# Folding attention vectors on TensorE, with ScalarE and TensorE in a written order, in a four-layer graph-attention kernel

## The chip, the cores and the metric

The kernel runs on one core of one Trainium2 chip. The metric is the device time of one execution in microseconds (us). A core has TensorE (PE: matrix products into PSUM), VectorE (DVE: elementwise work and reductions), ScalarE (ACT: functions of one operand, with a scale and a bias), GpSimd (POOL: elementwise work, and the issue of indirect DMAs, "gathers") and SyncE (SP: here only issues DMAs). Each engine runs its own list of instructions in order and waits on semaphores for the others. 16 DMA engines move data between HBM and SBUF.

## What is computed

There are 3327 nodes with 512 features and a sparse symmetric adjacency matrix with some 17 neighbours to a row. Four layers follow one another, each a layer norm with a ReLU, and a graph attention whose output is added to x. The first one, cut to what matters:

```python
h = jnp.maximum(_layernorm(x, axis=-1), 0.0)
h = (h @ W.T).reshape(n, 8, 64)                    # 8 heads of 64
e_src = jnp.einsum('nhd,hd->nh', h, a_src)
e_dst = jnp.einsum('nhd,hd->nh', h, a_dst)
e = leaky_relu(e_src[:, None, :] + e_dst[None, :, :], 0.2)
alpha = softmax(where(mask[:, :, None], e, -inf), axis=1)
x = x + jnp.einsum('ijh,jhd->ihd', alpha, h).reshape(n, 512)
```

The other layers differ in heads (4, 1, 8), in an elu, and in whether a node always attends to itself. The scores e_src and e_dst are linear in the normalised input, so the kernel "folds" the attention vectors into the weights: column j of W times a_src, summed over a head, is one more column of the weight matrix. A projection of 512 + 16 columns then gives features and scores at once.

## The kernel before, in words

Rows are padded to 3328 and cut into 26 tiles of 128 (`NT`).

**The list stage** (`tile_gat_stack`, lines 526 to 791) turns the dense adjacency matrix into neighbour lists, and projects all tiles for layer 0. For each tile t:

- SP loads the adjacency tile `a` (128x3328 int32, 1664 KB; three buffers; L697). GpSimd multiplies it by descending column numbers into `key` (L698; three buffers).
- VectorE adds a bonus to the diagonal (L702) and takes the 8 largest of each of 16 segments (L707). Between these it works off `pieces` of the tile before: the 40 largest overall (L662, L664), the count held (L635, `counted`), its one-hot row (L640, `sorted_in`), and later the place within it (L654, `placed`).
- ScalarE sums the adjacency tile (L704), copies the list out (L632, L633), and centres the row tile x of 128x512 with its variance (`centred_by_scalar`, L488 to L495). The row tile `vx` (five buffers) is loaded from ScalarE's own DMA queue (L726).
- TensorE turns the centred tile (`turned`, L454), ScalarE cuts it (`cut`, L461), TensorE projects it into `pv` (`projected`, L472; one PSUM buffer), GpSimd takes the root of the variance (`rooted`, L434), ScalarE scales `pv` by it into `vx` (L683, L685), and SP stores that row tile (528 KB) in the table `tabx` (L687). In `features` all of it is called for tile t-1 at the end of step t.
- TensorE also sums the one-hot rows into running counts (L642 to L646), which ScalarE copies to `sofar` (L649) for the next tile.

In step 1 the weights of layer 0 are loaded (`Weights`, L382 ff.), and all eight folds follow at once on VectorE: a product `prod` of 128x512 (L408) and a reduction of it (L410) each. The folds read the attention vectors broadcast over 128 partitions (`av`, L395).

```python
with tc.manual_schedule(engines={Pool, DVE}):
    for t in range(NT):
        ...
        if t == 1:
            while W.left:
                W.fold()
```

What sets the order: inside `manual_schedule` the engines named keep the order of the program text. The others (here ScalarE, TensorE and SP) are ordered by the compiler's own scheduler. After the last tile, VectorE ranks the rows by their counts (L738 to L750), and TensorE builds lists of gather indices (L789) with `low` and `spare` as scratch; `low` lives from the stage's start and is not used until then.

**The layers** (`tile_gat_lists`) go over tiles in steps of up to four neighbours (`GROUP`). In layer 0, each step's neighbours are gathered from `tabx` by GpSimd (L838), five steps ahead (`LOOK`, buffers `g`). `scored` makes the attention weights (L892 to L908), `group` multiplies features by them on VectorE (L931) and sums on TensorE (L936). A finished tile is normed, turned and projected by the weights of the next layer (L472). The next layer's weights `W` are folded on VectorE in steps 0, 1 and 2 of layer 0, three at a time (L1436 to L1438), and those of the layer after are loaded at step 16 of a layer.

Of the kernel before, what the change touches and what calls it, by code (L numbers as in the profile page):

```python
# [10 lines left out]
F32 = mybir.dt.float32  # L11
U8 = mybir.dt.uint8
BF16 = mybir.dt.bfloat16
I32 = mybir.dt.int32
AF = mybir.ActivationFunctionType
# [3 lines left out]
P = 128  # L19
# [361 lines left out]
class Weights:  # L381

    def __init__(self, nc, pool, work, l, ws, avs):
        F = ws[l].shape[0]
        HF, KC = F // 2, F // P
        self.l, self.H, self.D = l, HEADS[l], F // HEADS[l]
        self.nc, self.work, self.HF = nc, work, HF
        self.w = pool.tile([P, KC, 2, HF + 8], F32, name="w")  # L390
        self.av = pool.tile([P, 2, F], F32, name="av", bufs=1)
        for s in range(2):
            nc.sync.dma_start(self.w[:, :, s, :HF],
                              ws[l][:, s * HF:(s + 1) * HF].rearrange("(k p) n -> p k n", p=P))
            nc.sync.dma_start(self.av[:, s, :], bass.AP(tensor=avs[l].tensor, offset=avs[l].offset + s * F,  # L395
                                                        ap=[[0, P], [1, F]]))
        if self.H < 8:
            nc.vector.memset(self.w[:, :, :, HF + self.H:], 0.0)
        self.left = [(s, k) for s in range(2) for k in range(KC)]

    def fold(self):

# [46 lines left out]
def turned(nc, xn, ident, ps_t):  # L449

    KC = xn.shape[1] // P
    pt = ps_t.tile([P, KC, P], F32, name="pt")
    for k in range(KC):
        nc.tensor.transpose(pt[:, k, :], xn[:, k * P:(k + 1) * P], ident)  # L454
    return pt


def cut(nc, pt, work):

    hT = work.tile(list(pt.shape), F32, name="hT")  # L460
    nc.scalar.activation(hT, pt, AF.Relu)  # L461
    return hT


def projected(nc, W, hT, ps_v):

    KC = hT.shape[1]
    HF = KC * P // 2
    pv = ps_v.tile([P, 2, BANK], F32, name="pv")
    for s in range(2):  # L470
        for k in range(KC):
            nc.tensor.matmul(pv[:, s, :HF + 8], hT[:, k, :], W.w[:, k, s, :],  # L472
                             start=(k == 0), stop=(k == KC - 1))
    return pv
# [50 lines left out]


@with_exitstack
def tile_gat_stack(ctx: ExitStack, tc: tile.TileContext, x, adj, adjT, ws, avs, out):

# [32 lines left out]
    with ExitStack() as c1:  # L564
# [16 lines left out]

        fixed = ps_k.tile([P, BANK], F32, name="fixed")
        ahead, boost, bins, one = fixed[:, :P], fixed[:, P:2 * P], fixed[:, 2 * P:2 * P + BINS], fixed[:, 298:299]
        nc.scalar.activation(boost, ident, AF.Copy, scale=BOOST)
        ones = once.tile([P, P], F32, name="ones")
        upper = once.tile([P, P], F32, name="upper")
        limit = once.tile([P, BINS], F32, name="limit")
# [50 lines left out]
        def sorted_in(t):  # L638
            nonlocal sofar, count
            nc.vector.tensor_scalar(o[:, t, :], bins, held[:, t:t + 1], None, OP.is_equal)  # L640
            pn = ps_n.tile([P, BANK], F32, name="pn", bufs=1)
            nc.tensor.matmul(pn[:, :BINS], upper, o[:, t, :], start=True, stop=False)  # L642
            nc.tensor.matmul(pn[:, :BINS], ident, sofar, start=False, stop=True)
            count = ps_n.tile([P, BANK], F32, name="count", bufs=1)[:, :BINS]
            nc.tensor.matmul(count, ones, o[:, t, :], start=True, stop=False)
            nc.tensor.matmul(count, ident, sofar, start=False, stop=True)  # L646
            if t < NT - 1:
                sofar = once.tile([P, BINS], F32, name="sofar", bufs=2)
                nc.scalar.activation(sofar, count, AF.Copy)  # L649
            return pn  # L650

        def placed(t, pn):
# [24 lines left out]
            nc.vector.tensor_tensor(m1, own, L[:, :, 0], OP.not_equal)  # L677
            nc.vector.tensor_reduce(wrong[:, 1:2], m1, AX.X, OP.add)

        def features(t, vx, xn, ve):  # L680
            pv = projected(nc, W, cut(nc, turned(nc, xn, ident, ps_t), work), ps_v)
            rstd = rooted(nc, ve, small, half)
            nc.scalar.activation(vx[:, :ROW].rearrange("p (s n) -> p s n", s=2), pv[:, :, :ROW // 2], AF.Copy,  # L683
                                 scale=rstd)
            nc.scalar.activation(vx[:, ROW + F:].rearrange("p (s n) -> p s n", s=2), pv[:, :, ROW // 2 - 8:ROW // 2],  # L685
                                 AF.Copy, scale=rstd)
            nc.sync.dma_start(tabx[t * P:(t + 1) * P, :], vx)  # L687

        rows = [once.tile([P, 2 * ROW], F32, name=f"vx{i}") for i in range(5)]
        count, pieces, last, normed = None, [], None, None  # L690
        with tc.manual_schedule(engines={mybir.EngineType.Pool, mybir.EngineType.DVE}):
            for t in range(NT):
                a = apool.tile([P, NP], I32, name="a")
                key = kpool.tile([P, NP], I32, name="key")
                quarter = NP // 4 if t == 0 else NP
                for c in range(0, NP, quarter):
                    nc.sync.dma_start(a[:, c:c + quarter], adj[t * P:(t + 1) * P, c:c + quarter])  # L697
                    nc.gpsimd.tensor_tensor(key[:, c:c + quarter], a[:, c:c + quarter], keys[:, c:c + quarter], OP.mult)  # L698
                if t == 1:
                    W = Weights(nc, wpool, work, 0, ws, avs)  # L700
                dg = key[:, t * P:(t + 1) * P]
                nc.vector.tensor_add(dg, dg, boost)  # L702
                waste = once.tile([P, NP], mybir.dt.bfloat16, name="waste")
                nc.scalar.activation(waste, a, AF.Relu, accum_out=total[:, t:t + 1])  # L704
                cand = small.tile([P, SEGS * 8], F32, name="cand")
                for g in range(SEGS):
                    nc.vector.max(cand[:, g * 8:(g + 1) * 8], key[:, g * SEG:(g + 1) * SEG])  # L707
                    if g == SEGS // 2 and last is not None:
                        last()
                        last = None  # L710
                    elif g > 0 and pieces:
                        pieces.pop(0)()
                if t == 0:
                    constants()
                if t == 1:
                    while W.left:
                        W.fold()
                if t == 2:
                    own = late_constants()
                if t > 0:  # L720
                    last = then
                pieces, then = rest(t, cand)

                vx = rows[t % 5]
                xt = vx[:, ROW:ROW + F]
                nc.scalar.dma_start(xt, x[t * P:(t + 1) * P, :])  # L726
                if normed is not None:
                    features(*normed)
                normed = (t, vx, *centred_by_scalar(nc, xt, small, work))
            features(*normed)  # L730
            pieces[4:4] = [last]
            for piece in [*pieces, check, then]:
                piece()

        with tc.manual_schedule(engines={mybir.EngineType.Pool, mybir.EngineType.PE,
                                         mybir.EngineType.DVE, mybir.EngineType.Activation}):
# [63 lines left out]
def tile_gat_lists(ctx: ExitStack, tc: tile.TileContext, x, adj, ws, avs, out, ident, half, slots, L, low, spare, tabx, tabs):  # L800
# [48 lines left out]
    class Tile:  # L849


        def __init__(self, l, t, W):
            self.l, self.t, self.W = l, t, W

            first = GROUP - 1 if l == 0 else GROUP
            self.k0 = [0] + list(range(first, CAPS[t], GROUP))
            self.own = first - 1 if l == 0 else 0
            self.groups = []
# [138 lines left out]
        def cut(self):  # L997
            if self.W is not None:
                self.hT = cut(nc, self.pt, work)
# [365 lines left out]
    for l in range(NL):  # L1365
# [3 lines left out]
        with ExitStack() as c2:  # L1369
# [47 lines left out]
            for s in range(-1, at_end):  # L1417
                def do(place):
                    for piece in at.pop((s, place), []):
                        piece()  # L1420
                while fetched < min(len(steps), s + LOOK):
                    steps[fetched][0].fetch()
                    fetched += 1
                do("first")
                if s + 1 < len(steps):
                    steps[s + 1][0].scored(steps[s + 1][1])
                do("scored")
                if 0 <= s < len(steps):
                    tl, i = steps[s]
                    tl.group(i)  # L1430
                    if i == len(tl.k0) - 1:
                        tl.finish(s)
                do("last")
                if s == 16 and l + 2 < NL:
                    following = Weights(nc, wpool, work, l + 2, ws, avs)
                if l == 0 and s in (0, 1, 2):  # L1436
                    for _ in range(3):
                        W.fold()  # L1438
                if s >= 24 and s % 4 == 0 and following is not None:
                    following.fold()  # L1440
            scatter()
# [43 lines left out]
```

## Time and profile before

| what | us |
|---|---|
| median of 3 runs (lowest, highest) | 2424.75 (2415.73, 2427.66) |
| profiled execution: its own time | 2419.54 |
| its span, first to last instruction | 2417.8 |
| list stage: last key product ends | 241.1 |
| list stage: DMA of the ranks issued | 256.7 |
| first gather of layer 0 | 271.2 |

| engine | busy us | share |
|---|---|---|
| PE (products) | 2068.3 | 86% |
| DVE | 1885.1 | 78% |
| POOL | 1739.5 | 72% |
| ACT | 936.3 | 39% |

How to read what follows: a line of the timeline has start, duration, engine, line of the kernel, operation, output and input with shapes, and in brackets how long the engine sat idle ahead of it and what ended that. A line of waits has engine and line that waited, what it waited for, the sum in us, how often, and the longest. A line of the windows has busy us of PE, PE's weight loads, DVE, ACT and POOL in a stretch, the granted TensorE clock, the share of time that the DMA engines were busy, and GB/s. "SPq" and "ACTq" are DMA issues. The granted TensorE clock was 0.953 over the span.

### The profile page before, as it was taken

What the parts mean: (1) busy time and instruction counts of PE and PEld (TensorE: products, weight loads), DVE (VectorE), ACT (ScalarE), POOL (GpSimd) and SP (SyncE); (2) the same over time, 40 slices, a digit from 0 to 9 for tenths busy, and PEclk for the clock granted to TensorE, in tenths of its full rate; (3) what the DMA queues carried; (4) which work ended last, traced back from release to release, by engine and by line L of the source; (5) the groups of instructions that cost most, each with busy time, mean ns of one, the idle gap of its engine ahead of it and who ended that gap; (6) DMA issues with size and microseconds to landing.
All of it is one profiled execution on the core that took longest, in us unless ns stands there. A gap on an engine that the chain in (4) does not pass through costs nothing.

```text
span 2417.8 us, 27489 instructions
## 1 busy us (share of the span) xinstructions
PE 2068.3 (86%) x7298; PEld 1197.0 (50%) x7298; DVE 1885.1 (78%) x4857; ACT 936.3 (39%) x2528; POOL 1739.5 (72%) x1717
## 2 busy tenths in 40 slices
PE   2778779888988885898999987899898699999997
PEld 1656334444444432454455544456565465556653
DVE  7988788877777763888888884888878578888886
ACT  5777113434331111433333332544443444344430
POOL 7899267777777776766677772778778467777775
PEclk9988899999999997999999998999999899999999
DMA  5887569999998788887888884889887578888885
GB/s 227 316 299 248 153 192 299 276 299 282 286 283 237 234 231 241 242 245 235 234 261 255 256 237 141 270 262 283 268 248 240 161 226 256 250 243 246 252 241 176
DMA packets 260732, 594.23 MB, mean 246 GB/s; under 512 B 103699, under 2 KB 121107, under 8 KB 256214
## 3 DMA queue, kind: packets, MB, share of 16 engines
q0 software_dynamic: 124368, 432.13, 59.5%
q1 hardware_dynamic: 132454, 153.45, 19.6%
q10 hardware_dynamic: 3744, 6.82, 0.8%
q8 instruction: 59, 0.97, 0.2%
q14 instruction: 107, 0.88, 0.1%
HBM read 542.60 MB, written 49.65 MB: 245 GB/s over the span
## 4 chain that ended last, share of the span: by engine, by line
DVE 31%; DMA 17%; PE 16%; issue 13%; POOL 12%; ACT 9%; DVEq 0%; SPq 0%; ACTq 0%; POOLq 0%
DVE m L931 13%; POOL g L838 8%; DMA g<-tab,idxb 6%; PE bank L936 5%; DMA g<-tabx,twiceb 4%; PE pv L472 4%; PE whole L1173 3%; POOL key L698 3%; DVE bank L924 3%; ACT r L1280 2%; DMA g<-tab,idxa 2%; DVE room L1296 2%; DVE z L902 2%; ACT pw L903 2%; DVE z L900 1%
## 5 line engine op out<-in xcount | busy, mean ns | idle before, releaser
L936 PE MATMUL bank<-m,ident 128*128 128x512 f32 x2414 | 1128.0, 613 | 144.8 <-DVE m L931 144.3
L838 POOL DMA_INDIRECT g<-tab,idxb x712 | 683.1, 959 | 236.0 <-issue 162.0
L931 DVE TENSOR_TENSOR m<-g,pw 128x512 f32<-128x512 f32 x1207 | 752.2, 682 | 100.2 <-ACT pw L903 99.6
L936 PEld LDWEIGHTS bank<-m,ident 128*128 128x128 f32 x2414 | 448.7, 194 | 689.2 <-issue 314.6
L472 PE MATMUL pv<-w,hT 128*128 128x264 f32 x1664 | 431.5, 413 | 67.8 <-ACT hT L461 44.5
L903 ACT ACTIVATE pw<-z 128x32 f32<-128x32 f32 (+4 forms) x356 | 68.2, 191 | 988.9 <-DVE z L902 988.9
L472 PEld LDWEIGHTS pv<-w,hT 128*128 128x128 f32 x1664 | 331.7, 203 | 166.8 <-ACT hT L461 50.8
L838 POOL DMA_INDIRECT g<-tab,idxa x297 | 286.3, 964 | 165.0 <-issue 110.6
L838 POOL DMA_INDIRECT g<-tabx,twiceb x342 | 324.0, 947 | 106.0 <-issue 79.5
L1173 PE MATMUL whole<-ve,em 128*128 128x512 f32 x468 | 217.8, 612 | 16.3 <-DVE em L1152 11.2
L698 POOL TENSOR_TENSOR key<-a,keys 128x3328 int32<-128x3328 int32 (+1 forms) x29 | 189.3, 6530 | 16.3 <-DVE cand L707 11.8
L924 DVE SCALAR_TENSOR_TENSOR bank<-g,L,bank 128x512 f32<-128x512 f32 x243 | 183.3, 754 | 6.8
L900 DVE TENSOR_TENSOR z<-g,pw 128x32 f32<-128x32 f32 (+4 forms) x356 | 62.6, 176 | 152.1 <-DMA g<-tabx,twiceb 64.7
L1314 PEld LDWEIGHTS whole<-L,room 128*128 128x128 f32 x1248 | 147.5, 190 | 24.9 <-issue 19.1
L838 POOL DMA_INDIRECT g<-tabx,twicea x99 | 94.9, 959 | 78.5 <-issue 38.1
L1314 PE MATMUL whole<-L,room 128*128 128x130 f32 x1248 | 147.8, 274 | 0.0
L707 DVE MAX8 cand<-key 128x8 f32<-128x208 int32 x416 | 144.0, 364 | 0.1
L1173 PEld LDWEIGHTS whole<-ve,em 128*128 128x128 f32 x468 | 88.1, 196 | 109.2 <-issue 87.2
L1280 ACT ACTIVATE r<-low,L 128x384 f32<-128x384 f32 x208 | 121.2, 583 | 5.1
L454 PE MATMUL pt<-ident,xn 128*128 128x128 f32 x416 | 65.4, 281 | 35.4 <-ACT hT L461 13.6
L454 PEld LDWEIGHTS pt<-ident,xn 128*128 128x128 f32 x416 | 52.5, 145 | 68.6 <-issue 28.3
L931 DVE TENSOR_TENSOR bank<-g,pw 128x512 f32<-128x512 f32 x74 | 51.5, 696 | 37.4 <-ACT pw L903 36.6
(180 smaller groups left out, 2192.6 us busy)
## 6 DMA issues: line engine op xcount, KB each, us to landing
a<-in_adj SPq DMA_DIRECT2D x25, 1664.0 KB
tab<-v SPq DMA_DIRECT2D x78, 264.0 KB
ve<-tab SPq DMA_DIRECT2D x78, 264.0 KB
g<-tab SPq DMA_DIRECT2D x65, 264.0 KB
tabx<-vx SPq DMA_DIRECT2D x26, 528.0 KB
g<-tab,idxb POOLq DMA_INDIRECT x712, 4.0
low<-tab SPq DMA_DIRECT2D x52, 132.0 KB
spare<-tab SPq DMA_DIRECT2D x52, 132.0 KB
```

Source lines behind the costliest of these rows:

```text
L454: nc.tensor.transpose(pt[:, k, :], xn[:, k * P:(k + 1) * P], ident)
L472: nc.tensor.matmul(pv[:, s, :HF + 8], hT[:, k, :], W.w[:, k, s, :], start=(k == 0), stop=(k == KC - 1))
L698: nc.gpsimd.tensor_tensor(key[:, c:c + quarter], a[:, c:c + quarter], keys[:, c:c + quarter], OP.mult)
L707: nc.vector.max(cand[:, g * 8:(g + 1) * 8], key[:, g * SEG:(g + 1) * SEG])
L838: nc.gpsimd.indirect_dma_start(out=out_, out_offset=None, in_=table, in_offset=bass.IndirectOffsetOnAxis(ap=which, axis=0))
L903: nc.scalar.activation(self.wt[:, k0:k0 + n, :H], z, AF.Exp)
L924: nc.vector.scalar_tensor_tensor(acc, v, w, acc, OP.mult, OP.add)
L931: nc.vector.tensor_tensor(out_.rearrange("p (s h d) -> p s h d", s=2, d=D), v.rearrange("p s (h d) -> p s h d", d=D), wt[:, k0 + q, :H].re ...
L936: nc.tensor.matmul(self.po, ident, m[:, q, :], start=False, stop=(k0 + q == K - 1), skip_group_check=True)
L1173: nc.tensor.matmul(tl.po.rearrange("p (s m) -> p s m", s=2), e[:, q * P:(q + 1) * P], v.rearrange("p (s m) -> p s m", s=2)[:, :, :F // 2], ...
L1280: nc.scalar.activation(self.r[:, h, :], self.a[:, g, :], AF.Relu, bias=-1.0, scale=self.b[:, j, g:g + 1])
L1314: nc.tensor.matmul(dst, e[:, h, q * P:(q + 1) * P], mov, start=False, stop=(j == NT - 1), skip_group_check=True)
```

## The change

Three things are done.

1. The folds of layer 0 leave VectorE. A second copy of the weights in its own orientation (`w0t`, 512x512) and a sparse table made of the attention vectors (`s0`, 128 x 16) are new inputs, loaded into `low` in step 1 instead of the broadcast vectors. `Weights.multiply` forms 16 products on TensorE (four row blocks by four column blocks, four columns each) and four copies on ScalarE.
2. In the list stage TensorE and ScalarE too keep the order of the text, and the loop is rewritten for it: the row tile of t+1 is requested in step t (`given`), the root, the stores and the copy of the running count of tile t-2 stand after key product t (`rooted_row`, `stored`, `passed`), turning and projecting tile t-1 after these, and then sum and centring of tile t. The bonus `boost` is made first of all on ScalarE.
3. In layer 0 the next layer's weights are folded one piece a step in steps 1 to 8.

```diff
-    def __init__(self, nc, pool, work, l, ws, avs):
+    def __init__(self, nc, pool, work, l, ws, avs, turned=None):
...
+        if turned is not None:
+            room, wT, spread = turned
+            self.wT = room[:, :KC * F].rearrange("p (c f) -> p c f", c=KC)
+            self.spread = room[:, KC * F:KC * F + KC * 4].rearrange("p (c a) -> p c a", c=KC)
+            nc.sync.dma_start(self.spread, spread.rearrange("p (c a) -> p c a", c=KC))
+            nc.sync.dma_start(self.wT, wT.rearrange("(c p) f -> p c f", p=P))
...
+    def multiply(self, bank):
+
+        nc, HF, H = self.nc, self.HF, self.H
+        KC = self.wT.shape[1]
+        per = H // KC
+        pf = bank[:, :KC * 2 * H].rearrange("p (k s h) -> p k s h", k=KC, s=2)
+        for k in range(KC):
+            for c in range(KC):
+                nc.tensor.matmul(pf[:, k, :, c * per:(c + 1) * per], self.wT[:, c, k * P:(k + 1) * P],
+                                 self.spread[:, c, :2 * per].rearrange("p (s h) -> p s h", s=2), start=True, stop=True)
+        for k in range(KC):
+            nc.scalar.activation(self.w[:, k, :, HF:HF + H], pf[:, k], AF.Copy)
...
-            if t < NT - 1:
-                sofar = once.tile([P, BINS], F32, name="sofar", bufs=2)
-                nc.scalar.activation(sofar, count, AF.Copy)
...
+        def given(t):
+            if t < NT:
+                nc.scalar.dma_start(rows[t % 5][:, ROW:ROW + F], x[t * P:(t + 1) * P, :])
+
+        def rooted_row(t):
+            root_[t] = rooted(nc, centred_[t][1], small, half)
+
+        def stored(t):
+            vx, pv, rstd = rows[t % 5], pv_.pop(t), root_.pop(t)
...
+        def passed(t):
+            nonlocal sofar
+            if t < NT - 1:
+                sofar = once.tile([P, BINS], F32, name="sofar", bufs=2)
+                nc.scalar.activation(sofar, counts.pop(t), AF.Copy)
...
-        with tc.manual_schedule(engines={mybir.EngineType.Pool, mybir.EngineType.DVE}):
-            for t in range(NT):
...
-                if t == 1:
-                    while W.left:
-                        W.fold()
...
+        with tc.manual_schedule(engines={mybir.EngineType.Pool, mybir.EngineType.PE,
+                                         mybir.EngineType.DVE, mybir.EngineType.Activation}):
+            nc.scalar.activation(boost, ident, AF.Copy, scale=BOOST)
+            given(0)
+            for t in range(NT + 1):
+                if t < NT:
...
+                        nc.sync.dma_start(a[:, c:c + quarter], adj[t * P:(t + 1) * P, c:c + quarter])
+                        nc.gpsimd.tensor_tensor(key[:, c:c + quarter], a[:, c:c + quarter], keys[:, c:c + quarter], OP.mult)
+                    given(t + 1)
+                if t >= 2:
+                    rooted_row(t - 2)
+                    stored(t - 2)
+                    passed(t - 2)
                 if t == 1:
-                    W = Weights(nc, wpool, work, 0, ws, avs)
...
+                    W = Weights(nc, wpool, work, 0, ws, avs, (low.rearrange("p a b -> p (a b)"), *sums))
+                if t >= 1:
+                    hT = cut(nc, turned(nc, centred_[t - 1][0], ident, ps_t), work)
                 if t == 1:
...
+                    W.multiply(ps_i.tile([P, BANK], F32, name="pi"))
+                if t >= 1:
+                    pv_[t - 1] = projected(nc, W, hT, ps_v)
+                if t < NT:
+                    waste = once.tile([P, NP], mybir.dt.bfloat16, name="waste")
+                    nc.scalar.activation(waste, a, AF.Relu, accum_out=total[:, t:t + 1])
+                    centred_[t] = centred_by_scalar(nc, rows[t % 5][:, ROW:ROW + F], small, work)
...
+            rooted_row(NT - 1)
+            stored(NT - 1)
...
-                if l == 0 and s in (0, 1, 2):
-                    for _ in range(3):
-                        W.fold()
+                if l == 0 and 1 <= s <= 8:
+                    W.fold()
```

## The prediction

> **What bounds the kernel now.** I read the page first. VectorE 78%, GpSimd 72% and TensorE 86% busy are averages over stages with different limits, so I went to the stage that changes: the windows of 20 us, the waits in it, then its timeline engine by engine.
>
> From the windows (sum of busy us by engine, last three columns clock, DMA share, GB/s):
> ```profile
> 40.00:60.00 20.00, 8.26 (x15) 4.12 (x16) 19.69 (x33) 2.31 (x5) 11.07 (x4) 1.00 0.06 24
> 160.00:180.00 20.00, 15.41 (x71) 12.99 (x70) 16.89 (x85) 16.28 (x31) 18.65 (x5) 0.84 0.82 268
> 180.00:200.00 20.00, 15.41 (x64) 12.33 (x62) 18.23 (x89) 15.37 (x34) 16.66 (x6) 0.80 0.98 333
> ```
> See two regimes: a hole at 40 to 60 us in which only VectorE works and the DMA stands still, and then GpSimd, ScalarE and the DMA all close to full.
>
> The hole, from the timeline:
> ```profile
> 35.67 6.88 DVE L408 TENSOR_TENSOR prod<-w,av 128x512 f32<-128x512 f32 x1
> ...
> 43.31 7.36 DVE L408 TENSOR_TENSOR prod<-w,av 128x512 f32<-128x512 f32 x1
> ...
> 51.42 0.69 DVE L408 TENSOR_TENSOR prod<-w,av 128x512 f32<-128x512 f32 x1
> ...
> 62.84 7.27 POOL L698 TENSOR_TENSOR key<-a,keys 128x3328 int32<-128x3328 int32 x1 [11.77 <-DVE cand L707]
> ```
> The eight folds of layer 0 hold VectorE from 29.41 to 55.64. Three of the products take 2.6 to 7.4 us instead of 0.69, each while GpSimd multiplies a key tile (from 24.25, 34.52 and 42.93, 7.2 to 7.5 us each). VectorE frees no key buffer meanwhile, and GpSimd, three tiles ahead, then stands 11.77 us.
>
> The rest of the stage, from the waits between 60 and 240 us and GpSimd's timeline:
> ```profile
> POOL key L698 <- DVE cand L707: 11.8, 1, 11.8
> POOL root L434 <- ACT ve L495: 11.4, 6, 4.6
> ACT waste L488 <- DMA vx<-in_x: 10.9, 8, 2.3
> ```
> ```profile
> 173.58 7.26 POOL L698 TENSOR_TENSOR key<-a,keys 128x3328 int32<-128x3328 int32 x1
> 180.80 0.55 POOL L434 TENSOR_TENSOR root<-ve,half 128x1 f32<-128x1 f32 x1
> 181.32 7.25 POOL L698 TENSOR_TENSOR key<-a,keys 128x3328 int32<-128x3328 int32 x1
> 188.53 0.54 POOL L434 TENSOR_TENSOR root<-ve,half 128x1 f32<-128x1 f32 x1
> 189.04 7.23 POOL L698 TENSOR_TENSOR key<-a,keys 128x3328 int32<-128x3328 int32 x1
> 199.61 0.55 POOL L434 TENSOR_TENSOR root<-ve,half 128x1 f32<-128x1 f32 x1 [3.34 <-ACT ve L495]
> ```
> GpSimd alone needs 7.73 us a tile (key 7.26, root, gaps); where it takes longer, the root of the tile just ahead waits for ScalarE's variance, and ScalarE waited for a row load. From key(3) at 34.52 to key(25) at 233.80 are 199.3 us for 22 tiles, 9.06 each. VectorE needs 7.03 (62.68 to 69.71).
>
> The start of layer 0, GpSimd's timeline:
> ```profile
> 292.72 0.94 POOL L838 DMA_INDIRECT g<-tabx,twicea  x1 [0.30 <-issue]
> 303.39 0.94 POOL L838 DMA_INDIRECT g<-tabx,twicea  x1 [9.72 <-issue]
> ...
> 310.79 0.94 POOL L838 DMA_INDIRECT g<-tabx,twicea  x1 [2.58 <-DVE prod L408]
> 317.90 1.24 POOL L838 DMA_INDIRECT g<-tabx,twicea  x1 [6.17 <-issue]
> ```
> A gather is issued every 1.25 us, and from 325 to 900 us nearly without a gap (79 in each 100 us), so layer 0 goes at that pace. Before it gathers stand: their buffers wait for steps of VectorE, and three folds lie behind steps 0 and 1, two behind step 2.
>
> **The change, part by part.** Sums are against the profiled execution: 2419.54 us, its span 2417.8 plus 1.74 around it. The runs' median is 5.2 above it; the mean of the four times shown is 2421.9, and I subtract from that.
>
> *Folds of layer 0 leave VectorE.* 26.2 us of its work go. GpSimd is next. In their place stand 16 products of 128x4 on TensorE. Nearest row: the 128x41 products of L642 to L646 at 28.5 us, four in 1.9 us, 0.48 each, so 7.6 us; small because only four columns, so at least perhaps 4, at most 16 x 0.62 = 9.9 taken singly. I take 7.6. TensorE is empty there (7 of 20 us busy from 20 to 40), but ScalarE's order now waits for them: behind the four copies (some 0.2 each) stand the sum over adjacency tile 1, the centring of tile 1 and the list of tile 0. With wT landed near 20.5, products end at 28, copies at 28.7, the sum at 31.7. It frees the buffer of adjacency tile 4, whose load lands by 39.5; key(4) is due at 42.3. Hidden with 3 us left; if wT came 5 us late, 2 us would be lost once.
>
> *DMAs.* 0.5 MB of broadcast vectors go, 1.05 MB of wT and a small table come: +0.5 MB, 1.6 us at 333 GB/s. But four row tiles (1.05 MB) were loaded in the first 3.2 us, and now two come ahead of adjacency tile 2: -0.5 MB. I keep key(3) at 34.52, bounds -1 to +2.
>
> *Orders fixed.* The root of tile t-2 now follows key(t), a tile later than before, and rows are requested a tile ahead on ScalarE's queue. The 11.4 us of root waits go: variance(t-2) ends before key(t) begins. Who is late next? ScalarE's list for a tile is 0.76 (two stores) + 0.15 + 0.47 + 3.05 + 2.35 (centring) + 0.25 = 7.0; it starts 0.55 after key(t), when the root is there, so it fits into 7.73. Queued behind that wait is the adjacency sum, and behind this the load three tiles on (rival C). VectorE waits for none of it: the products of its counts come from TensorE, after 3.4 to 3.8 us of projection, and are used a tile later.
>
> *The DMA.* A tile moves 1664 + 528 + 256 KB = 2.507 MB. The fullest window gives 333 GB/s, 7.53 us a tile. The Trainium skill, DMA: Bandwidth & Descriptors, Specifications, puts a core's share of the memory at about 358 GB/s: 7.00 us, and GpSimd would have 0.7 us of air. By the row it has 0.2, and the mean of 60 to 220 us is 305, 8.2 us. I go by the fullest window, since the idle stretches were waits that go, and add 0.17 for two resources that run so close: 7.9 us. Then key(3) to key(25) is 173.8, a gain of 25.5 (29.2 at 7.73, 18.5 at 8.22).
>
> *End of the stage.* Counts of tile 24 come 7.6 us after the last key; ScalarE's copy of them now stands ahead of the last transposed tile, so the last projection ends 12.1 after it, and the count of tile 25 behind it starts at 12.1 instead of 11.0. Loss 1.2 (bounds 0 and 3). The last row store lands some 4 us later, 10 us ahead of its gathers.
>
> *Layer 1's folds over steps 1 to 8.* The work stays 8 x 1.43 us. Walked through with the rows' times, step groups now end at 302.6, 305.9, 310.4, 315.4, 320.1, 324.8; gathers of step 9 go out at 320.5 instead of 329.0; then the later folds eat some back: gathers of step 13 at 340.6 instead of 345.3, and from there it is continuous as before. Gain 4.7. Against it speaks the Trainium skill, SBUF — State Buffer, SBUF: two separate sides: a VectorE instruction with two SBUF inputs locks the port pair that GpSimd needs[...]. By the rule each product could hold up a gather by its 0.69: 8 x 0.69 = 5.5, and the gain is -0.8. The rows: gathers beside folds took 1.07, 1.14 and 1.24 instead of 0.95, 0.2 more. I take 0.7 in all: gain 4.0, bounds -0.8 and 8.5. Layer 2's vectors on SP's queue, which waited for the last fold (319.79), move to about 341; the next on that queue is a row store at 359. The first projection that reads these folds is at 349.98.
>
> Sum: 25.5 - 1.2 + 4.0 = 28.3; 2421.9 - 28.3 = 2393.6, I say 2393.
>
> **Rivals.**
> A, as above, 57%: 7.73 to 8.05 us a tile and the bounds of the folds give 2384 to 2403. Another 5%: better than that.
> B, the DMA sets the pace, 20%: at 8.22 to 8.6 us a tile the gain falls to 21.3 to 12.9, 2400 to 2409. For it: share 0.98 in one window. Against it: three tiles in a row at 7.73 from 165.84 to 189.04.
> C, slower, 11%: the ring of adjacency buffers. The load of tile t+3 waits for ScalarE's sum of tile t, now behind root, stores and copy: 5.4 us after key(t). Three tiles take 12.7 us plus the load's time L. Up to L = 10.5 GpSimd doesn't notice; at 14.5 nothing is gained in the stage; slower by 0.5% from 16.5; at 18 the pace is 10.2 and the time 2445. For it: a row load of 0.26 MB took 9.14 us in the chain at 122.44, behind bigger ones. Against it: the load alone is 5.1 us, store and rows 2.4 more, and at a slow pace the queue is empty.
> D, the hole closes but as much comes back elsewhere, 7%: 9 us a tile, within 12 us of before.
>
> **Numbers.** A measurement here tells about 0.5% (12 us) from no change: faster below 2412.6. Faster 57 + 5 + 20 = 82%, same 7%, slower 11%. The range takes A and B, 2383 to 2410.
>
> **What would show it.** Right: no L408 product before layer 0; keys 7.7 to 8.1 us apart from key(3); key(25) at about 208; no root waiting for ve; ScalarE over 85% busy there; the gap ahead of the sixth step's gathers stays, those ahead of the seventh and eighth shrink. B: keys waiting for adjacency loads with DMA share 0.95 or more. C: the same waits with a DMA share below 0.85. Fold step wrong: gathers beside folds near 1.6 us. Wrong as a whole if key(25) comes after 225 us.

## The result, and the profile after

| | before | after |
|---|---|---|
| median of the runs (lowest, highest), us | 2425.71 (2415.73, 2427.66) of 4 | 2392.57 (2389.91, 2393.57) of 4 |
| profiled execution: its time, its span | 2419.54, 2417.8 | 2393.57, 2391.8 |
| key(3) starts, key(25) starts | 34.52, 233.80 | 33.79, 203.97 |
| last key product ends | 241.07 | 211.29 |
| first gather of layer 0 | 271.24 | 244.83 |

The ratio is 0.987, 95% interval 0.9841 to 0.9898. The forecast of 2393 met the median to 0.4 us, partly by luck: three terms of its sum were off, in both directions, and most of what follows is about those. The granted clock was 0.95 over the span, as before.

First the windows of the changed kernel (columns as before: PE, weight loads, DVE, ACT, POOL, clock, DMA share, GB/s):
```profile
40.00:60.00 20.00, 13.57 (x64) 10.87 (x63) 17.67 (x87) 17.77 (x39) 20.00 (x7) 0.91 0.87 330
160.00:180.00 20.00, 14.98 (x80) 11.96 (x79) 18.54 (x93) 18.70 (x37) 20.00 (x5) 1.00 0.91 324
180.00:200.00 20.00, 14.83 (x71) 11.89 (x71) 18.39 (x90) 17.94 (x35) 20.00 (x7) 0.91 0.91 341
```
The hole is gone (GpSimd, too, had worked 11.07 us in it), and GpSimd is busy 20.00 of 20 us in each of the eight windows from 40 to 200. One engine is full and the others are not: VectorE 92% and ScalarE 91% over the eight, the DMA share 0.87 to 0.96 at 313 to 341 GB/s.

GpSimd's timeline and, after it, the waits from 40 to 205 us say the same instruction by instruction:
```profile
180.75 7.33 POOL L733 TENSOR_TENSOR key<-a,keys 128x3328 int32<-128x3328 int32 x1
187.97 0.62 POOL L455 TENSOR_TENSOR root<-ve,half 128x1 f32<-128x1 f32 x1
188.48 7.35 POOL L733 TENSOR_TENSOR key<-a,keys 128x3328 int32<-128x3328 int32 x1
```
```profile
DVE key L754 <- POOL key L733: 16.0, 22, 3.2
...
ACT vx L709 <- POOL root L455: 9.0, 17, 0.7
```
From key(3) to key(25) are 170.18 us for 22 tiles, 7.74 each: key, root and gaps, nothing else. No line of the waits has GpSimd as the one that waits; VectorE and ScalarE now wait for it, 0.5 to 0.7 us a tile. Before, GpSimd waited for both.

The start of the stage, where the new products stand (all engines):
```profile
19.04 6.96 PE L417 MATMUL pi<-low 128*128 128x4 f32 x32 [3.67 <-DMA low<-in_w0t]
23.48 7.25 POOL L733 TENSOR_TENSOR key<-a,keys 128x3328 int32<-128x3328 int32 x1 [3.06 <-DMA a<-in_adj]
26.04 0.41 ACT L420 ACTIVATE w<-pi 128x16 f32<-128x16 f32 x4 [8.98 <-PE pi L417]
```
The 16 products show as 32 records and take 6.96 us. ScalarE stands 8.98 us for them, and the adjacency sum follows behind the copies. No later key pays for it.

The end of the stage (all engines again), after the last key has ended at 211.29:
```profile
213.15 3.00 ACT L749 ACTIVATE waste<-a 128x3328 bf16<-128x3328 int32 x1
...
219.71 0.60 ACT L482 ACTIVATE hT<-pt 128x512 f32<-128x512 f32 x1
...
220.37 5.41 PE L493 MATMUL pv<-w,hT 128*128 128x264 f32 x16 [1.14 <-ACT hT L482]
...
226.19 0.20 DVE L671 SCALAR_TENSOR_TENSOR junk<-pn,o 128x41 f32<-128x41 f32 x1 [3.07 <-PE pn L663]
...
226.63 0.24 DVE L777 TENSOR_TENSOR_SCAN base<-ones,count 128x41 f32<-128x41 f32 x1 [0.24 <-PE count L666]
```
ScalarE does the sum, the centring and the list of the last tile after the last key, so the last projection starts at 220.37, 9.1 us after it, and takes 5.41 us. TensorE keeps the order of the text, so the count of tile 25 waits behind it until 225.6. The scan of the bins starts 15.3 us after the last key's end, where it was 12.4 before.

The projection before it took only 3.83 us for the same 16 products. The windows of the two differ in the granted clock, 1.00 and 0.70:
```profile
213.33:217.16 3.83, 3.83 (x16) 2.96 (x16) 3.83 (x23) 3.80 (x5) 0.00 (x0) 1.00 0.35 141
220.37:225.78 5.41, 5.41 (x19) 4.40 (x19) 2.47 (x14) 0.47 (x2) 0.00 (x0) 0.70 0.24 100
```
5.41 x 0.70 is 3.8, so 1.6 us of the later scan are the clock of this execution and not the order. Two other executions with the same order at the end (order_only of run 3 and change_again of run 11) had a clock of 1.00 there: their last projection takes 3.83 us, and the scan starts 13.8 us after the last key.

The start of layer 0, gathers on GpSimd's timeline:
```profile
277.32 0.94 POOL L877 DMA_INDIRECT g<-tabx,twicea  x1 [10.02 <-ACT pw L942]
...
284.67 1.23 POOL L877 DMA_INDIRECT g<-tabx,twicea  x1 [1.04 <-issue]
...
310.18 0.94 POOL L877 DMA_INDIRECT g<-tabx,twicea  x1 [4.72 <-issue]
...
328.56 0.94 POOL L877 DMA_INDIRECT g<-tabx,twicea  x1 [2.00 <-ACT pw L942]
```
The gap of 6.17 us that the folds left before shrank, and two others came, of 4.72 and 2.00 us. Beyond 1.25 us a gather, the 42 gathers from the 18th to the 60th (the first one counted as 0, here and below) took 10.66 us more before and 8.75 after, counted in the traces.

### The profile page after: what moved, and what is told of

Read it like the earlier page. It is cut to its first block, busy times and chain, and to the rows that moved or that the text cites. A ratio compares the mean times of both kernels' runs of the same rounds, so it can differ in the third digit from the quotient of the medians.

```text
span 2391.8 us, 27546 instructions
## 1 busy us (share of the span) xinstructions
PE 2072.4 (87%) x7330; PEld 1203.4 (50%) x7330; DVE 1854.1 (78%) x4841; ACT 944.5 (39%) x2532; POOL 1740.9 (73%) x1717
## 4 chain that ended last, share of the span: by engine, by line
DVE 22%; DMA 17%; PE 11%; issue 11%; POOL 10%; ACT 7%; DVEq 0%; SPq 0%; POOLq 0%; ACTq 0%
DVE m L970 10%; POOL g L877 9%; DMA g<-tab,idxb 9%; DMA g<-tabx,twiceb 4%; PE whole L1212 4%; PE bank L975 3%; DMA g<-tab,idxa 3%; PE pv L493 2%; ACT r L1319 2%; DVE bank L963 2%; DVE room L1335 2%; ACT pw L942 1%; DVE z L941 1%; DVE z L939 1%; ACT L L1330 1%
## 5 line engine op out<-in xcount | busy, mean ns | idle before, releaser
L493 PE MATMUL pv<-w,hT 128*128 128x264 f32 x1664 | 425.3, 413 | 46.6 <-ACT hT L482 43.5
L493 PEld LDWEIGHTS pv<-w,hT 128*128 128x128 f32 x1664 | 336.7, 204 | 144.0 <-ACT hT L482 51.2
L475 PE MATMUL pt<-ident,xn 128*128 128x128 f32 x416 | 66.0, 283 | 29.1 <-ACT xn L511 14.3
```

## The experiments

Four groups were run, each beside the kernel before on its own chip. In groups 1 and 4 the kernel before took 2421.46 and 2423.48 us. In groups 2 and 3 it took 2905.25 and 2925.85: on those chips the list stage runs as here (7.74 us a tile), but the layers are slower. There times are compared only within a group or through the ratio, with the changed kernel itself at 0.9812; and how layer 0 behaves there says little about the first chip.

**1. The spreading undone** (group 1).

```diff
-                if l == 0 and 1 <= s <= 8:
-                    W.fold()
+                if l == 0 and s in (0, 1, 2):
+                    for _ in range(3):
+                        W.fold()
```

> The list stage of the change, with layer 1's folds back behind steps 0, 1 and 2 of layer 0. Theory of the prediction (gathers set the pace from step 9 on, so a gap that folds open is lost for good): some 4 us more than the changed kernel's 2392.6, so 2396 to 2397, and gathers that are 3 to 5 us later, counted from the first gather, at the 40th and still at the 500th. Rival (VectorE is the bound until about step 12 and has the same work in either order): 2392 to 2393, gathers later by some us at the 25th to 40th and by under 1 us from the 100th on.

Measured: 2393.96 us (2390.72 to 2398.10), ratio 0.989 (0.9866 to 0.9913). The 43rd gather comes 73.72 us after the first (spread 70.77, before 74.05), the 100th 144.96 (143.78), the 500th 648.43 (648.06; before 648.19). The spreading is ahead by 3.0 us at the 43rd gather and by 0.4 at the 500th. It brings nothing that the time shows.

**2 and 3. Each half of the list-stage change alone** (group 1). First only the products on TensorE, in the kernel before:

```diff
-                    W = Weights(nc, wpool, work, 0, ws, avs)
+                    W = Weights(nc, wpool, work, 0, ws, avs, (low.rearrange("p a b -> p (a b)"), *sums))
...
-                    while W.left:
-                        W.fold()
+                    W.multiply(ps_i.tile([P, BANK], F32, name="pi"))
```

> The kernel before with only the folds of layer 0 moved to TensorE; orders of ScalarE and TensorE left to the scheduler, layer 1's folds as before. Theory (two separate gains in the list stage: the stall of 11.8 us behind the folds, and the pace of 8.6 us a tile, which the order sets): key(5) at about 51 instead of 62.8, then 8.4 to 8.7 us a tile, 2412 to 2414. Rival (the folds had upset the whole pipeline, the order does nothing): 7.7 to 7.9 us a tile, 2396 to 2398.

Then only the written order, with the folds on VectorE in step 1:

```diff
-                if t == 1:
-                    W.multiply(ps_i.tile([P, BANK], F32, name="pi"))
-                if t >= 1:
+                if t >= 2:
                     pv_[t - 1] = projected(nc, W, hT, ps_v)
...
+                    if t == 1:
+                        while W.left:
+                            W.fold()
+                        pv_[0] = projected(nc, W, hT, ps_v)
```

> The changed kernel with layer 0's folds back on VectorE after the lists of step 1, and the first projection after them. Theory of key buffers (GpSimd waits for VectorE alone): key(5) at about 63 instead of 49.3, then 7.73 a tile, 13 to 14 us more than the changed kernel, 2406. Theory of the ring (ScalarE stands at the stores of tile 0 until the projection at 57 us, the sum of adjacency tile 2 ends at 62, and the load of tile 5 lands at 70): key(5) at about 70, 20 to 22 us more, 2413.

Measured: 2417.44 us (2413.51 to 2424.32), ratio 0.999 (0.9976 to 1.0004), for the products; 2407.36 (2406.23 to 2411.46), ratio 0.995 (0.9934 to 0.9967), for the order. Against 2421.46 beside them that is 4 (the interval of the ratio includes 1) and 14, while both halves together, run 1 in the same group, give 27.5. The halves do not add up. The timeline shows why, for the products alone (GpSimd, then ScalarE and SP's queue):
```profile
61.40 7.22 POOL L710 TENSOR_TENSOR key<-a,keys 128x3328 int32<-128x3328 int32 x1 [10.46 <-DMA a<-in_adj]
```
```profile
34.58 2.97 ACT L716 ACTIVATE waste<-a 128x3328 bf16<-128x3328 int32 x1
...
50.81 0.34 SPq L699 DMA_DIRECT2D tabx<-vx  x1
51.24 0.38 SPq L709 DMA_DIRECT2D a<-in_adj  x1
```
The stall of 11.77 us for VectorE has become one of 10.46 for the load of adjacency tile 5. Its buffer is free from 37.6, when the sum of tile 2 ends. But in the compiler's order the load stands on SP's queue behind a row store, which waits for ScalarE's scaling until 50.8, and goes out only at 51.24. So key(5) comes at 61.40 and not at the 51 of the theory; from there on a tile takes 8.56 us, which the theory had. For the order alone, all engines:
```profile
41.45 7.37 DVE L429 TENSOR_TENSOR prod<-w,av 128x512 f32<-128x512 f32 x1
...
55.27 0.70 ACT L709 ACTIVATE vx<-pv,root 128x528 f32<-128x528 f32 x1 [28.33 <-PE pv L493]
...
62.10 0.55 POOL L455 TENSOR_TENSOR root<-ve,half 128x1 f32<-128x1 f32 x1 [13.84 <-ACT ve L516]
...
68.38 7.27 POOL L733 TENSOR_TENSOR key<-a,keys 128x3328 int32<-128x3328 int32 x1 [5.73 <-DMA a<-in_adj]
```
Here the folds end near 54 us, ScalarE waits 28.33 us for the projection that reads them, the centring waits behind it, the root waits for that and the next load for the sum. Key(5) comes at 68.38, near the 70 of the theory of the ring, and from there a tile takes 7.74 us. The first gather is 17.3 us later than in the changed kernel; the time is only some 14 more, because 3.4 us come back between the 900th and the 975th gather (more on that in run 12). So the order alone gives the pace but keeps the stall, and the products alone only change what the stall waits for; each needs the other for the hole to close.

**4. The slow products with one operand elsewhere** (group 1). As run 3, but ScalarE copies the broadcast vector to a PSUM bank, and the product reads it there:

```diff
+                        for s in range(2):
+                            va = ps_i.tile([P, BANK], F32, name="pi")
+                            nc.scalar.activation(va, W.av[:, s, :], AF.Copy)
+                            for _ in range(F // P):
+                                W.fold(va)
```

> As the kernel with the folds back on VectorE in step 1, but the broadcast attention vectors are copied to PSUM first, so that each product reads one operand from SBUF. Theory (products of 2.6 to 7.4 us come of two operands from SBUF beside GpSimd's key product): all eight products near 0.7 us, folds over within 13 us, key(5) at about 55, some 6 us more than the changed kernel, 2398 to 2399. Rival (they waited for something else, data or a semaphore): some products stay at 2.6 to 7.4 us and the time is that of the kernel with folds on VectorE.

Measured: 2398.83 us (2393.15 to 2402.12), ratio 0.9908 (0.9881 to 0.9934). All engines:
```profile
32.97 7.21 POOL L733 TENSOR_TENSOR key<-a,keys 128x3328 int32<-128x3328 int32 x1
...
34.37 0.69 DVE L429 TENSOR_TENSOR prod<-w,pi 128x512 f32<-128x512 f32 x1 [0.51 <-DVE w L431]
...
53.83 7.26 POOL L733 TENSOR_TENSOR key<-a,keys 128x3328 int32<-128x3328 int32 x1 [4.94 <-DMA a<-in_adj]
```
All eight products take 0.66 to 0.69 us, this one in the midst of a key product, where with both operands in SBUF they took up to 7.37. So the 26 us of folds were 11.4 of work and the rest a block by GpSimd's product. The Trainium skill, SBUF — State Buffer, SBUF: two separate sides, states that a VectorE instruction with two SBUF inputs and a GpSimd instruction that reads SBUF shut each other out; here a trace shows it, and that one operand in PSUM lifts it. Key(5) and the time are as the theory had them. Most of the change's gain is to be had with the folds left on VectorE, in the written order: 22.6 of the 27.5 us in this group, with 4.94 lost to one load. The step from run 3's order alone is 8.5.

**5. Two adjacency buffers instead of three** (group 2), the ring of rival C made to bind:

```diff
-        apool = c1.enter_context(tc.tile_pool(name="adj", bufs=3))
+        apool = c1.enter_context(tc.tile_pool(name="adj", bufs=2))
```

> The changed kernel with two adjacency buffers instead of three. Theory of the ring, which the prediction named as the slow rival (key, root, stores and sum 5.4 us, then the load, 8.0 us by the page, then the key product, 7.3): 20.7 us for two tiles, 10.3 a tile, 57 us more over 22 tiles, 2449; with a load of 6.5 us, since the queue is emptier, 9.6 a tile and 2434. Rival (loads have air and the third buffer is not needed): 7.7 to 7.9 a tile, 2392 to 2396.

Measured: 2904.50 us (2890.46 to 2927.31), ratio 1.0006 (0.9969 to 1.0042). A tile takes 9.73 us, the first gather comes at 290.38 (three buffers, in group 3, 243.59). A window, and a wait from 60 to 240 us:
```profile
160.00:180.00 20.00, 13.16 (x56) 10.45 (x56) 14.24 (x70) 14.19 (x28) 16.04 (x5) 0.76 0.68 249
```
```profile
POOL key L733 <- DMA a<-in_adj: 17.1, 9, 4.2
```
GpSimd waits for loads while the DMA is busy 0.68 of the time: the signature that the prediction gave for C, absent from the changed kernel. Another 22.8 us of its waits are put down to VectorE in the same view, but VectorE itself stands 51.8 us for keys there, so these are taken to be loads too. The ring formula gave 10.3 us a tile with a load of 8.0 and 9.6 with one of 6.5. It holds, and with three buffers it has air.

**6. No root on GpSimd** (group 2). The root is replaced by a constant, so the rows are not scaled by their deviation.

```diff
-            root_[t] = rooted(nc, centred_[t][1], small, half)
+            root_[t] = half
```

> The changed kernel with the root left out in the list stage: a constant stands in its place, so layer 0's features have another scale; adjacency lists are unchanged. Theory (GpSimd alone sets 7.73 us a tile, DMA and ScalarE have air): pace 7.25 to 7.3, the last key 10 us earlier, 2382 to 2383. Rival (the DMA is nearly as late: 2.507 MB at 330 to 340 GB/s): pace 7.4 to 7.6 with keys that wait for adjacency loads, 2385 to 2389. If ScalarE is next (7.0 us of work): the same pace without such waits.

Measured: 2847.73 us (2843.91 to 2870.14), ratio 0.9813 (0.9759 to 0.9866). The first gather comes at 236.34, 7.2 us earlier than with the root (243.59 in group 3). A tile takes 7.45 us, 0.29 less, where the root and its gap are 0.5. A window:
```profile
160.00:180.00 20.00, 16.70 (x72) 13.29 (x71) 19.34 (x97) 18.07 (x34) 20.00 (x3) 0.83 0.94 342
```
So GpSimd set the pace: less work there, and the stage is shorter. But 7.45 is the rival's pace, not the 7.25 to 7.3 of GpSimd alone, so the next limits lie 0.3 us below: VectorE is busy 19.34 of 20, the DMA moves 342 GB/s. Keys waited for loads 2.9 us in all, in waits of at most 1.1, some 0.13 a tile. Which of the limits takes the rest was not separated.

**7. The tail mended** (group 2): turning, projection and store of the last tile moved behind the last counts.

```diff
-                if t >= 1:
+                if 1 <= t < NT:
                     pv_[t - 1] = projected(nc, W, hT, ps_v)
...
+            pv_[NT - 1] = projected(nc, W, cut(nc, turned(nc, centred_[NT - 1][0], ident, ps_t), work), ps_v)
             rooted_row(NT - 1)
```

> The changed kernel with the turning, projection and store of the last tile moved behind its counts, on all engines. Theory (the count of tile 25 stands 3 us behind the last projection on TensorE, and everything after it shifts): the last key to the ranks as before the change, 15.6 us, the first gather some 3 us earlier, 2389. Rival (the index lists or the last row store set the end anyway): the first gather no earlier than 33 us after the last key, 2392 to 2393.

Measured: 2869.68 us (2861.57 to 2878.38), ratio 0.989 (0.9829 to 0.995). The scan starts at 225.36, 13.7 after the last key instead of 15.3, and yet the first gather comes at 245.42, 33.8 after the last key's end (the changed kernel 33.5). All engines:
```profile
226.90 5.40 PE L493 MATMUL pv<-w,hT 128*128 128x264 f32 x16 [0.69 <-ACT hT L482]
...
232.45 0.15 DVE L800 TENSOR_REDUCE worst<-pn 1x1 f32<-1x3 f32 x1 [2.22 <-PE pn L798]
```
The projection now stands ahead of another small product that VectorE waits for (L798), 2.22 us: the wait has a new place. But the projection ran at a granted clock of 0.70, and the one of tile 24 took 6.87 us instead of 3.83. At a clock of 1.00 the last one would end 1.6 us sooner and leave some 0.6 of the wait (an estimate from 5.40 and 3.83). On another chip with the same end (both_mends, below) the scan starts 12.1 us after the last key and the first gather comes 31.8 after it, against 13.8 and 32.3 of change_again beside it, though both of its last two projections had a clock of 0.69. So the move brings the scan forward; what it is worth to the first gather, a fraction of a microsecond or some 2 (an estimate: the 0.4 measured and the 1.6), is not settled.

**8 to 11. Layer 1's folds off VectorE, in another way** (groups 2 and 3). The score columns of layer 1 set to zero, no folds; then its vectors folded on TensorE in steps 2 to 5; then both mends together; and the changed kernel itself, for comparison.

```diff
-                if l == 0 and 1 <= s <= 8:
-                    W.fold()
...
+    nc.vector.memset(following.w[:, :, :, F // 2:F // 2 + following.H], 0.0)
+    following.left = []
```

> The changed kernel without the folds of layer 1 at all: the score columns of its weights are set to zero, so layer 1's attention is uniform; the rest is unchanged. Theory (VectorE bounds steps 0 to 12 of layer 0, and the gain of spreading failed because the work stayed): 8 x 1.43 = 11.4 us less work lets the gathers run at 1.25 us from the sixth step on; the 100th gather comes 135 us after the first instead of 143.8, and the whole gains 7 to 9 us, 2384 to 2386. Rival (the first steps are bounded by gathers or loads, or layer 0 gives it back later): under 2 us, 2391 to 2393.

```diff
-                if l == 0 and 1 <= s <= 8:
-                    W.fold()
+                if l == 0 and 3 <= s <= 6:
+                    W.copied(folded, s - 3)
+                if l == 0 and 2 <= s <= 5:
+                    W.multiplied(folded, s - 2)
```

> The changed kernel with layer 1's vectors folded by TensorE too: 16 products of 128x2x1 columns in steps 2 to 5 of layer 0 and four copies on ScalarE in steps 3 to 6, from a second copy of the weights loaded into the scratch after the index lists; no fold on VectorE before layer 2's. Theory (VectorE bounds the first steps; TensorE and ScalarE have room): as without the folds, the 100th gather 135 to 137 us after the first, 6 to 9 us less than the changed kernel, 2384 to 2386. Rival (products wait for the late load, and ScalarE's copies hold up the attention weights): 0 to 3 us less, 2390 to 2393, with waits of ScalarE for the copies' products.

> Both: layer 1's vectors folded by TensorE, and the last tile's projection behind its counts. If the two are independent, one in the list stage and one in layer 0: the sum of both, 9 to 12 us less than the changed kernel, 2381 to 2383. If the shorter tail only brings the wait forward (an index list or a store), no more than the fold alone, 2384 to 2386.

> The changed kernel itself once more, for the runs beside it on the same chip: 2390 to 2394 by every theory.

Measured: no folds 2850.63 us (2845.74 to 2865.44), ratio 0.9824 (0.9769 to 0.9878); TensorE's folds 2878.48 (2854.88 to 2884.20), ratio 0.9834 (0.9801 to 0.9866); both mends 2889.54 (2868.36 to 2900.41), ratio 0.9849 (0.981 to 0.9887); the change again 2875.60 (2858.57 to 2878.77), ratio 0.9812 (0.9778 to 0.9845). None of them can be told from the change. Without folds the 55th gather was 3.1 us ahead of the changed kernel's, and the lead was gone by the 70th. From 400 to 500 us these kernels start 58 to 61 gathers where the first chip starts 79, and VectorE is busy 60 to 65 us instead of 79: it has room there in which folds may hide; this was argued and not tested. Inconclusive for the first chip, so one of them was run once more, and it came to a chip like the first.

**12. No folds in layer 1, again** (group 4).

> The changed kernel with the score columns of layer 1 set to zero instead of folded (the nine folds and their three copies are left out, so the attention scores of layer 1 are all alike and the output differs), a second look. If the place of the folds is repaid within layer 0 because the gathers are the pace there (theory after the earlier comparisons), the lead of some 3 us at the 55th gather is gone by the 200th and the time is that of the changed kernel within 5 us (ratio to the kernel before 0.985 to 0.989 where that takes about 2425). If VectorE sets the pace through layer 0, all nine folds' time (some 9 us) stays to the end: ratio about 0.983 there.

(There are eight folds, not nine as the text says, and 8 x 1.43 is 11.4 us.) Measured: 2380.52 us (2378.73 to 2385.77), ratio 0.9834 (0.9812 to 0.9856). That is 12 us less than the changed kernel by the medians, which come from two chips, and 8.7 by the ratios, whose intervals overlap; the gathers, counted, are the better measure. GpSimd's timeline:
```profile
276.76 0.94 POOL L877 DMA_INDIRECT g<-tabx,twicea  x1 [9.69 <-ACT pw L942]
278.01 0.95 POOL L877 DMA_INDIRECT g<-tabx,twicea  x1 [0.30 <-DVE m L970]
```
After the one gap of 9.69 us there is none of more than 0.3 up to 330 us. The theory that the place of the folds is repaid because the gathers set the pace falls, and VectorE's stands. Time beyond 1.25 us a gather, from the 18th to the 60th: 10.66 before, 10.30 folds together, 8.75 spread, 0.01 without folds. The lead is 9.1 us at the 60th gather and still 9.8 at the 500th. So eight folds cost nearly their whole 11.4 us of VectorE, in either of the two places. The profiled execution gains 3.6 more between the 900th and the 975th gather. Both kernels of runs 2 and 3 gain 3.4 to 3.8 in the same place, with all their folds, so this is put down to the execution and not to the folds.

## Why the prediction was right

**The list stage: right, mis-sized by 4.3.** The term was 25.5 us at 7.9 us a tile; measured are 29.1 at 7.74, and key(3) came 0.73 earlier, 29.8 together. The choice that failed is "and add 0.17 for two resources that run so close". GpSimd and the DMA did run close (7.53 by the fullest window, 7.73 by GpSimd), and after key(3) no key waited for a load. The prediction's other end, 29.2 at 7.73, was the right one. The bounding engine was named rightly: run 6 shortens the stage by shortening GpSimd's work.

**The products on TensorE: right.** 7.6 us taken, 6.96 measured; wT came at 19.0 and not 20.5; the copies were hidden.

**No root waits; VectorE waits for nothing that matters: right**, by the waits of 40 to 205 us.

**The end of the stage: right in kind; the size was nearly right, and the clock made it larger.** 1.2 was taken, 33.54 - 30.17 = 3.4 measured. The step that failed is "the last projection ends 12.1 after it"; it ends 14.5 after. 0.8 of the 2.4 us is ScalarE. The walk went from the count of tile 24 by its copy to the last transposed tile, and left out that the copy stands behind ScalarE's own work on tile 25. In the written order that work stands behind the root and the stores, and these behind the last key: it begins at 213.15, and the projection starts 9.1 us after the key instead of 8.3. The other 1.6 is the projection, 5.41 us where 3.8 was taken, at a granted clock of 0.70. Where the clock was 1.00 the scan came 1.4 us later than before, beside the 1.2 of the term.

**Layer 1's folds: wrong.** The gain of 4.0 was there at the 43rd gather (3.3 measured against 4.7 walked through, before contention), then fell: 1.6 us at the 60th, 2.0 at the 100th, 0.8 at the 200th, 0.35 at the 300th and 0.13 at the 500th. The step that failed is "from there it is continuous as before". The walk stopped at step 13, and the last folds, in steps 6 to 8, still held up gathers five steps later (2.00 us at 328.56). More than that, the prediction itself wrote that the work stays 8 x 1.43 us and that the gathers wait there for steps of VectorE, and did not draw the conclusion. VectorE was busy 43 of the 50 us from 280 to 330, so a new order of its work can win only from the 7 us of gaps; it won 1.9. Run 1 shows the indifference, run 12 that the time is VectorE's. Of those 1.9 us another 1.1 went between the 100th and the 200th gather; that was not followed further. Gathers beside folds cost more than the 0.7 us taken and less than the 5.5 of 0.69 a product: four took 1.23 to 1.38 us instead of 0.95, 1.5 more in all.

The sum: 29.8 - 3.4 + 0.1 = 26.5, beside 26.0 between the spans; forecast 28.3, taken from a mean over runs 2.4 above the profiled execution. The list stage gave 4.3 more than forecast, the end and the folds 2.2 and 3.9 less. The medians differ by 33 because the profiled execution of before lay 6.2 below its median, and that of after 1.0 above. So the hit has two parts of luck: the errors of the terms came to only 1.8, and a gain that was 4.8 too small by the medians was taken from a start that was 3.8 too low.

**The rivals.** B, the DMA at 8.22 us or more: did not come, no key waits with a DMA share of 0.95 or more. C, the ring: not in the changed kernel, where an adjacency load took 8.0 us from issue to landing, below the 10.5 from which the prediction let it matter. Run 5 brings it about and gives 9.73 us a tile. D, the hole closes and comes back elsewhere: that is what the products do alone (run 2), in part the order too (run 3), and what the whole avoids.

Still open: whether folding layer 1's vectors on TensorE gains up to the 9.8 us of run 12 on a chip like the first (it was run only where layer 0 may hide the folds); what set the granted clock at the end of the stage; and why the change gains 50 us on the third group's chip. The list stage would explain some 26 of these if the kernel before runs it there as on the first chip, of which no trace was kept.

## What to carry to other kernels

Before work is moved within a stretch, ask which engine is full there: if it is the one that does the work, a new place brings only the gaps that it fills, and only taking the work away brings its time. When an order is fixed by hand, write down for the last iteration, too, what stands behind the releasing instruction on each engine, because there nothing follows that hides it. Two halves of a change that free the same ring, here a slow VectorE stretch and an order that lets loads and stores stand behind late ScalarE work, may each gain little alone: judge them together. Before a longer instruction is put down to its place in the program, look at the granted clock of its own window.

## What the hardware showed beside that

- A VectorE product of two SBUF operands beside a GpSimd product took up to 7.37 us; with one operand in PSUM 0.69. Four gathers that GpSimd began 0.1 to 0.2 us after such a product began took 1.23 to 1.38 us instead of 0.95; two that had begun before it (287.45 and 298.26) took 0.94 and 0.95.
- The same 16 products of 128x264 blocks (L493) took 3.83 us in windows with a granted clock of 1.00, 5.41 and 5.51 in windows with 0.70 and 0.69 (the last tile and the one at 205.60), and 6.78 in one with 0.56 (run 1, at 205.78). The product of time and clock is 3.8 each time.
- Chips differ by stage: the same kernel took 2392.57 and 2875.60 us on two of them. The list stage, with loads by SP, was alike to 1.3 us (first gather 244.83 and 243.59), and the clock of the last projection alone makes 1.6. In the layers the second chip moved 221 GB/s instead of 278 from 400 to 500 us, at a DMA share of 0.74 instead of 0.91. What holds the gathers there, these traces do not tell.
